# Transposing layer 1's input on VectorE and moving norms in a four-layer graph network

## The chip, the cores and the metric

The kernel runs on one core of a Trainium2 chip. The metric is the device time of one execution in microseconds. TensorE (PE) multiplies matrices and transposes through PSUM, VectorE (DVE), ScalarE (ACT) and GpSimd (POOL) do the elementwise work, and SyncE (SP) issues nearly all DMA transfers. Each of them works through its own queue of instructions in order.

## The reference

64 graphs of 256 nodes, 256 features, fp32. Four layers, each of the form "norm of x plus layer of x":

```python
x = _layernorm(x + L0(x, adj))   # gated recurrence over the 256 nodes
x = _layernorm(x + L1(x, adj))   # relu(D^-1/2 adj D^-1/2 (x W^T + b))
x = _layernorm(x + L2(x, adj))   # attention with relu projections, one head, mask adj
x = _layernorm(x + L3(x, adj))   # attention with 8 heads, mask adj > 0, output projection

def _layernorm(x, axis=-1, eps=1e-5):
    m = jnp.mean(x, axis=axis, keepdims=True)
    v = jnp.var(x, axis=axis, keepdims=True)
    return (x - m) / jnp.sqrt(v + eps)
```

The norms have no weights of their own.

## The kernel before

The recurrence of layer 0 runs first, for all 64 graphs together, and writes its states to `Hd` in HBM, laid out [node, graph, feature]. Then `_layers` does the residual and norm of layer 0 and the whole of layers 1 to 3, graph by graph. In it a graph's x is one tile `y` of 128 partitions by 2 by 256: node c*128 + p lies in partition p, half c.

`class Graph` holds one graph's steps. The steps of five graphs are interleaved by a list written out by hand, `ROUND`. In round t the letters stand for graphs at different depths: L is graph t+1, A is t, B is t-1, C is t-2 and E is t-3. So a graph passes the letters L, A, B, C, E in five rounds. The list sets the order on every engine, because the scheduler is switched off there (`tc.manual_schedule()`). At the head of each round the loads of graph t+2 are issued on SP:

```python
for t in range(-1, B + 3):
    if 0 <= t + 2 < B:
        graphs[t + 2].load()
    for step in ROUND:
        who, name, *args = step.split(".")
        b = t - "LABCE".index(who) + 1
        if 0 <= b < B:
            getattr(graphs[b], name)(*map(int, args))
```

The steps that matter here:

- `load` (L1033 to L1045): x into `xin`, adj into `ad`, adj once more in 32-wide blocks into `az` (eight DMAs of 32 KB), and the state from Hd into `y`. In `az` the blocks lie so that VectorE's transpose of 32 by 32 blocks (`adT_v`, L1076) gives the transposed adj.
- `residual_0` (L1049): y += xin on GpSimd.
- `norm_a`, `norm_b` (L949 to L961): mean and variance on VectorE, the power -1/2 on GpSimd (L953), `shift` = -mean * rstd on VectorE (L959), then y * rstd + shift in two halves on ScalarE (L961). The argument is the number of the layer whose sum is normed.
- `xT` (L987, L1094): the four 128x128 transposes of y on TensorE, and one copy of 128x512 out of PSUM on ScalarE. It is done for the inputs of layers 1, 2 and 3.
- `t` (L1099) and `g`: layer 1. t = xT^T W1^T + b1, then g, adj times t, with the degrees' scales, and y += g on GpSimd (L1108).
- `qk2`, `v2`, `s2` (L1140), `exp2`, `w2`, `pT2`, `f2`: layer 2.
- `bias_3` (L1176, L1177): y is written to `Yd` in HBM by a DMA, then b3 is added to y on GpSimd, in place. `Yd` is read only by a fallback that runs if a sum in layer 3 is out of range.
- `qk3`, `s3`, `v3`, `o3`, `d3`, `f3`: layer 3. `s3` issues 8 matmuls and then, four times, an add of the mask on VectorE (L1204), an exponential on ScalarE (L1205) and a sum of two halves on GpSimd (L1207, `p3s`). `o3` takes row sums from `p3s` (L1221) and the product with v (L1230).
- `store` (L1256): the DMA of y to the output.

PSUM tiles of the tag "mm" rotate through four buffers; `y` has seven buffers, `xin` and `az` three, `ad` four. A DMA takes one of eight semaphores in turn, and so waits for the DMA eight places ahead of it.

Of the kernel before, what the change touches and what calls it, by code (L numbers as in the profile page):

```python
# [9 lines left out]
F32 = mybir.dt.float32  # L10
BF16 = mybir.dt.bfloat16
AF = mybir.ActivationFunctionType
ALU = mybir.AluOpType
# [6 lines left out]
P = 128  # L20
# [891 lines left out]
def _layers(tc, ident, Hd, Yd, x, adj, weights, out):  # L912
# [8 lines left out]
    nc = tc.nc  # L921
    nat, W2, W3, b1_r, b2_r, b3_r, cols = weights
    B, N, D = x.shape
# [5 lines left out]
    with ExitStack() as ctx:  # L929
        const = ctx.enter_context(tc.tile_pool(name="l_const", bufs=1))  # L930
        W1T = const.tile([P, 2, D], F32, name="W1T")
# [7 lines left out]
        io = ctx.enter_context(tc.tile_pool(name="l_io", bufs=3))  # L939
# [4 lines left out]
        def norm_a(y, t):  # L944

            mv = small.tile([P, 2, 2], F32, tag="mv", name=f"mv_{t}")
            for c in range(2):
                st = small.tile([P, 6], F32, tag="st", name=f"st_{t}_{c}")
                nc.vector.bn_stats(st, y[:, c, :])  # L949
                nc.vector.bn_aggr(mv[:, c, :], st)  # L950
            rstd = small.tile([P, 2], F32, tag="rstd", name=f"rstd_{t}")
            nc.vector.tensor_scalar(rstd, mv[:, :, 1], EPS, None, ALU.add)  # L952
            nc.gpsimd.tensor_tensor(rstd, rstd, mhalf, ALU.pow)  # L953
            return mv, rstd

        def norm_b(y, mv, rstd, t):

            shift = small.tile([P, 2], F32, tag="shift", name=f"shift_{t}")
            nc.vector.scalar_tensor_tensor(shift, mv[:, :, 0], -1.0, rstd, ALU.mult, ALU.mult)  # L959
            for c in range(2):  # L960
                nc.scalar.activation(  # L961
                    y[:, c, :], y[:, c, :], AF.Identity, bias=shift[:, c:c + 1],
                    scale=rstd[:, c:c + 1],
                )

        def bank(name, shape=(P, 2, D)):
            return ps.tile(list(shape), F32, tag="mm", name=name, bufs=4)

        for c in range(2):
# [2 lines left out]
                nc.tensor.transpose(pt[:, k, :], nat[:, c, k * P:(k + 1) * P], ident)  # L972
            nc.vector.tensor_copy(W1T[:, :, c * P:(c + 1) * P], pt)

        nc.vector.tensor_copy(bv, cols[:, 4, :].unsqueeze(2).to_broadcast([P, 2, P]))
        pb = bank("bv3_ps", (P, D))
        for k in range(2):
# [4 lines left out]
        def flipped(src, t):  # L982

            pt = bank(f"tr_{t}")
            for a in range(2):
                for c in range(2):
                    nc.tensor.transpose(  # L987
                        pt[:, a, c * P:(c + 1) * P], src[:, c, a * P:(a + 1) * P], ident
                    )
            return pt  # L990

        def product(lhsT, rhs, t):

            pm = bank(f"mm_{t}")
            for c in range(2):
                for k in range(2):
                    nc.tensor.matmul(  # L997
                        pm[:, c, :], lhsT[:, k, c * P:(c + 1) * P], rhs[:, k, :],
                        start=(k == 0), stop=(k == 1),
                    )  # L1000
            return pm

        def new(tag, t, bufs=2, shape=(P, 2, D)):
            return work.tile(list(shape), F32, tag=tag, name=f"{tag}_{t}", bufs=bufs)

        def rows(b):
            return b.unsqueeze(1).to_broadcast([P, 2, D])
# [14 lines left out]
        class Graph:  # L1022
# [7 lines left out]
            def load(self):  # L1030
                b = self.b
                self.xin = io.tile([P, 2, D], F32, tag="xin", name=f"xin_{b}")
                nc.sync.dma_start(self.xin, x[b].rearrange("(c p) d -> p c d", p=P))  # L1033
                self.ad = io.tile([P, 2, N], F32, tag="ad", name=f"ad_{b}", bufs=4)
                nc.sync.dma_start(self.ad, adj[b].rearrange("(c p) m -> p c m", p=P))
                self.az = io.tile([P, 2, 8, 32], F32, tag="az", name=f"az_{b}", bufs=3)
                for j in range(4):
                    for a in range(2):
                        at = a * P + j * 32
                        nc.sync.dma_start(  # L1040
                            self.az[j * 32:(j + 1) * 32, a],
                            adj[b, :, at:at + 32].rearrange("(i r) c -> r i c", r=32),
                        )
                self.y = io.tile([P, 2, D], F32, tag="y", name=f"y_{b}", bufs=7)
                nc.sync.dma_start(self.y, Hd[:, b, :].rearrange("(c p) d -> p c d", p=P))  # L1045


            def residual_0(self):
                nc.gpsimd.tensor_add(self.y, self.y, self.xin)  # L1049

            def norm_a(self, l):
                self.mv = norm_a(self.y, f"{l}_{self.b}")

            def norm_b(self, l):
                norm_b(self.y, *self.mv, f"{l}_{self.b}")
# [37 lines left out]
                self.xT_sb = new(f"xT{l}", self.b)  # L1093
                nc.scalar.copy(self.xT_sb, pt)  # L1094

            def t(self):
                pm = product(self.xT_sb, W1T, f"t_{self.b}")
                self.t_sb = new("t", self.b)
                nc.vector.tensor_add(self.t_sb, pm, rows(b1_r))  # L1099

            def g(self):
                pm = product(self.adT_sb, self.t_sb, f"g_{self.b}")
# [155 lines left out]


        ROUND = """  # L1260
            A.xT.1 B.xT.2 E.o3 E.d3.0 B.qk2.0 C.norm_b.2 E.d3.1
            A.t B.qk2.1 B.v2 L.residual_0 B.masks L.degrees_a
            L.adT_v E.f3 L.degrees_b C.xT.3 L.adT_s A.g C.bias_3 L.norm_a.0
            C.qk3.0 C.qk3.1 E.norm_a.3 A.norm_a.1 L.norm_b.0 B.s2 B.exp2
            C.s3.0 C.v3 B.w2
            B.pT2 E.norm_b.3 E.store A.norm_b.1 C.s3.1 B.f2
            B.norm_a.2
        """.split()
        graphs = [Graph(b) for b in range(B)]
# [1 line left out]
# [6 lines that stand above are left out]
# [146 lines left out]
def kernel(ctx: ExitStack, tc: tile.TileContext, ins, out):  # L1423
# [25 lines left out]
    )  # L1449
    Yd = dram.tile([B, P, 2, D], F32, name="Yd")  # L1450
    found = _layers(tc, ident, Hd, Yd, x, adj, weights, out)
    with tc.If(found > 0):
        _layer_3(tc, ident, Yd, adj, l3, out)
# [36 lines left out]
```

## Time and profile before

| what | us |
|---|---|
| median of three runs | 3351.38 (3345.61 to 3360.14) |
| the profiled execution | 3353.51 |
| its span, first to last instruction | 3351.7 |
| recurrence ends, first load of `_layers` | 1475.4 |
| period of a round in the layers | 28.34 |

The page gives busy times of each engine and the span in 40 slices of about 84 us: the recurrence fills slices 1 to 17, the layers the rest. In the layers TensorE's clock was granted in full. A timeline lists instructions by their start; the number behind the start is the time from its first to its last instruction, where several are merged (x2, x4). "SPq" is the time in which SP issues a DMA, not the time of the transfer.

### The profile page before, as it was taken

To read this page: it belongs to the slowest core of one execution; us is meant where nothing else is said; L and a number is where in the kernel's file an instruction comes from. 1 tells how busy PE (TensorE), PEld (TensorE's weight loads), DVE (VectorE), ACT (ScalarE), POOL (GpSimd) and SP (SyncE) were. 2 spreads that over 40 slices of the span, in tenths; PEclk is the share of its full clock that TensorE was granted. 3 is DMA by queue.
4 is the path that set the end of the run, shared out by engine and by line. 5 is a ranking of instruction groups with operands and counts; after the bars stand their busy time and mean duration, and the time that the engine had idled before them with its cause. 6 is when DMAs were issued, how large, how long until landed. Compare 5 with 4: busy or idle time off the path is not lost.

```text
span 3351.7 us, 78940 instructions
## 1 busy us (share of the span) xinstructions
PE 3131.6 (93%) x28584; PEld 2311.5 (69%) x28584; DVE 2554.5 (76%) x7381; ACT 1838.6 (55%) x4754; POOL 1845.0 (55%) x2165
## 2 busy tenths in 40 slices
PE   5799998998879998969999999999999999999997
PEld 4566665555545555547888888888888888888885
DVE  3487777776667878856888888888888888888885
ACT  0155554544445544535666666666666666666664
POOL 2377777766667878833444444444444444444443
PEclk7899999999999999989999999999999999999999
DMA  9856685788877675241221211122222222222210
GB/s 292 247 161 156 168 194 152 179 198 207 204 181 178 163 174 152 65 105 47 56 57 54 57 56 54 54 55 58 57 58 58 58 57 58 57 58 58 58 33 20
DMA packets 528608, 364.62 MB, mean 109 GB/s; under 512 B 246620, under 2 KB 494568, under 8 KB 522984
## 3 DMA queue, kind: packets, MB, share of 16 engines
q1 hardware_dynamic: 510520, 342.63, 39.6%
q10 hardware_dynamic: 17696, 16.91, 1.5%
q8 instruction: 229, 3.75, 0.5%
q14 instruction: 163, 1.34, 0.1%
HBM read 240.78 MB, written 99.61 MB: 102 GB/s over the span
## 4 chain that ended last, share of the span: by engine, by line
PE 77%; DMA 8%; DVE 7%; issue 2%; SPq 2%; ACT 2%; POOL 1%; DVEq 0%; ACTq 0%; POOLq 0%
PE mm L997 14%; PE rc L605 6%; PE rc L597 4%; PE s L1195 4%; PE mm_2f L997 3%; PE mm_3v L997 3%; PE mm_3f L997 3%; PE mm_2v L997 3%; PE late L521 3%; PE mm_t L997 3%; PE mm_2s L997 3%; PE mm_g L997 3%; PE mm_2w L997 3%; PE o L1230 3%; DVE ACC L630 3%; PE o L1221 3%
## 5 line engine op out<-in xcount | busy, mean ns | idle before, releaser
L1207 POOL TENSOR_TENSOR p3s<-p 128x256 f32<-128x256 f32 x512 | 358.9, 733 | 364.7 <-ACT p L1205 364.6
L630 DVE SCALAR_TENSOR_TENSOR ACC<-keep,S,ACC 128x128 f32<-128x128 f32 x1712 | 479.1, 343 | 16.9 <-POOL ACC L876 11.2
L997 PE MATMUL mm<-xT,weights 128*128 128x256 f32 x2048 | 483.7, 384 | 2.7 <-ACT xT L1094 2.7
L997 PEld LDWEIGHTS mm<-xT,weights 128*128 128x128 f32 x2048 | 386.0, 191 | 79.9 <-issue 25.5
L1204 DVE TENSOR_TENSOR p<-s,neg 128x512 f32<-128x512 f32 x512 | 317.6, 682 | 118.2 <-PE s L1195 118.2
L667 POOL TENSOR_TENSOR ACC<-ACC,far 128x384 f32<-128x384 f32 (+1 forms) x313 | 372.1, 1189 | 24.5
L663 POOL TENSOR_TENSOR far<-hs,S 128x384 f32<-128x384 f32 (+1 forms) x313 | 304.7, 973 | 4.7
L1205 ACT ACTIVATE p<-p 128x512 f32<-128x512 f32 x512 | 292.4, 626 | 1.6 <-DVE p L1204 1.6
L961 ACT ACTIVATE y<-y,shift,rstd 128x256 f32<-128x256 f32 x512 | 272.9, 599 | 26.6 <-DVE shift L959 22.7
L597 PE MATMUL rc<-WxT,xqT 128*64 128x256 f32 x2048 | 274.8, 390 | 1.1 <-issue 1.1
L1119 ACT ACTIVATE qk<-mm,weights 128x256 f32<-128x256 f32 x256 | 107.5, 471 | 301.9 <-PE mm L997 301.9
L805 POOL TENSOR_TENSOR ready<-ACC,dinv 128x128 f32<-128x128 f32 x255 | 102.1, 400 | 304.7 <-DVE ACC L630 304.2
L1108 POOL TENSOR_TENSOR y<-y,g 128x512 f32<-128x512 f32 x64 | 81.0, 1266 | 301.8 <-issue 301.8
L1244 DVE RECIPROCAL rT<-o 128x256 f32<-128x256 f32 x128 | 223.7, 1748 | 0.3 <-PE o L1221 0.2
L949 DVE BATCH_NORM_STATS2 st<-y 128x6 f32<-128x256 f32 x512 | 209.6, 409 | 13.1 <-POOL y L1108 10.3
L521 PE MATMUL late<-Hw,An 64*32 64x256 f32 x3840 | 166.7, 400 | 42.1 <-DMA Hw<-hs 18.8
L605 PE MATMUL rc<-WhT,rT 128*64 128x128 f32 x2048 | 172.5, 290 | 35.6 <-DVE rT L828 33.2
L824 ACT ACTIVATE rs<-rc 128x128 f32<-128x128 f32 x256 | 71.1, 278 | 245.0 <-PE rc L605 245.0
L605 PEld LDWEIGHTS rc<-WhT,rT 128*64 128x64 f32 x2048 | 109.1, 138 | 133.2 <-DVE rT L828 110.8
L953 POOL TENSOR_TENSOR rstd<-rstd,mhalf 128x2 f32<-128x2 f32 x256 | 173.8, 697 | 47.9 <-DVE rstd L952 34.6
L1066 POOL TENSOR_TENSOR dis<-dis,mhalf 128x2 f32<-128x2 f32 x64 | 44.9, 702 | 273.2 <-DVE dis L1065 261.8
L605 PE MATMUL rc<-WhT,xpT 128*64 128x128 f32 x2048 | 169.4, 286 | 18.1 <-ACT xpT L614 18.1
(162 smaller groups left out, 7255.4 us busy)
## 6 DMA issues: line engine op xcount, KB each, us to landing
xX<-in_x_dram ACTq DMA_DIRECT2D x16, 1024.0 KB
Us<-xu SPq DMA_DIRECT2D x64, 256.0 KB
xq<-in_x_dram SPq DMA_DIRECT2D x64, 256.0 KB
ACC<-Us SPq DMA_DIRECT2D x32, 512.0 KB
Es<-eu SPq DMA_DIRECT2D x64, 256.0 KB
early_sb<-Es SPq DMA_DIRECT2D x32, 512.0 KB
xin<-in_x_dram SPq DMA_DIRECT2D x64, 256.0 KB
ad<-in_adj_dram SPq DMA_DIRECT2D x64, 256.0 KB
```

Of the source, the lines that this page charges most:

```text
L521: nc.tensor.matmul(pb[g][q * T:(q + 1) * T, e, :], An[rows, b].rearrange("p u s -> p (u s)"), Hw[rows, b, :], start=True, stop=True,)
L597: nc.tensor.matmul(G[o * B:(o + 1) * B], xqT[a, i // 2][:, i % 2, kc, h * B:(h + 1) * B], WxT[:, kc, o, gates], start=False, stop=False, s ...
L605: nc.tensor.matmul(G[o * B:(o + 1) * B], hT[:, kc * B:(kc + 1) * B], WhT[:, kc, o, g], start=False, stop=(kc == 1), skip_group_check=True,)
L630: nc.vector.scalar_tensor_tensor(acc[:, 0, :], keep[:, j % 2, :], s, acc[:, 0, :], ALU.mult, ALU.add)
L663: nc.gpsimd.tensor_mul(tmp[:, 0:count, :], hs.unsqueeze(1).to_broadcast(shape), s.unsqueeze(2).to_broadcast(shape),)
L667: nc.gpsimd.tensor_add(acc, acc, tmp[:, 0:count, :])
L961: nc.scalar.activation(y[:, c, :], y[:, c, :], AF.Identity, bias=shift[:, c:c + 1], scale=rstd[:, c:c + 1],)
L997: nc.tensor.matmul(pm[:, c, :], lhsT[:, k, c * P:(c + 1) * P], rhs[:, k, :], start=(k == 0), stop=(k == 1),)
L1204: nc.vector.tensor_add(p, s_ps[i], self.neg3)
L1205: nc.scalar.activation(p, p, AF.Exp, scale=ISQ)
L1207: nc.gpsimd.tensor_add(both, p[:, 0, :], p[:, 1, :])
L1244: nc.vector.reciprocal(rT, o_ps[:, 1, :])
```

## The change

Layer 1 no longer takes its transposed input from TensorE. The state and x are loaded a second and third time, in 32-wide blocks (`hz`, `xz`, eight DMAs each); GpSimd adds them (`residual_0`), and VectorE transposes the sum (`turn_0`) into `xT0`, before any norm. The norm is applied behind the product: W1 has its mean over the input features taken off once, at the start, so that the mean of x drops out, and t is the product times rstd, plus b1, in two halves with a scale per partition. y itself is still normed (`norm_b.0`), for the residual sum.

In ROUND the step A.xT.1 goes, A.t becomes A.t_a and A.t_b, L.turn_0 is new behind A.norm_b.1, and E.norm_b.3 with E.store move from ahead of A.norm_b.1 to behind C.s3.1.

```diff
+        mean = const.tile([P, P], F32, name="mean")
+        nc.gpsimd.memset(mean, 1.0 / D)
+        pb = bank("w1_mean", (P, D))
+        for k in range(2):
+            nc.tensor.matmul(pb, mean, W1T[:, k, :], start=(k == 0), stop=(k == 1))
+        for k in range(2):
+            nc.vector.tensor_sub(W1T[:, k, :], W1T[:, k, :], pb)
...
-                self.az = io.tile([P, 2, 8, 32], F32, tag="az", name=f"az_{b}", bufs=3)
-                for j in range(4):
-                    for a in range(2):
-                        at = a * P + j * 32
-                        nc.sync.dma_start(
-                            self.az[j * 32:(j + 1) * 32, a],
-                            adj[b, :, at:at + 32].rearrange("(i r) c -> r i c", r=32),
-                        )
+                self.az, self.hz, self.xz = (
+                    io.tile([P, 2, 8, 32], F32, tag=f"{s}z", name=f"{s}z_{b}", bufs=3)
+                    for s in "ahx"
+                )
+                for to, of in ((self.az, adj[b]), (self.hz, Hd[:, b, :]), (self.xz, x[b])):
+                    for j in range(4):
+                        for a in range(2):
+                            at = a * P + j * 32
+                            nc.sync.dma_start(
+                                to[j * 32:(j + 1) * 32, a],
+                                of[:, at:at + 32].rearrange("(i r) c -> r i c", r=32),
+                            )
...
             def residual_0(self):
                 nc.gpsimd.tensor_add(self.y, self.y, self.xin)
+                nc.gpsimd.tensor_add(self.hz, self.hz, self.xz)
+
+            def turn_0(self):
+                self.xT0 = new("xT0", self.b)
+                nc.vector.transpose(
+                    self.xT0.rearrange("p a m -> p (a m)"),
+                    self.hz.rearrange("p a i c -> p (a i c)"),
+                )
...
-            def t(self):
-                pm = product(self.xT_sb, W1T, f"t_{self.b}")
+            def t_a(self):
+                self.t_ps = product(self.xT0, W1T, f"t_{self.b}")
+
+            def t_b(self):
+
                 self.t_sb = new("t", self.b)
-                nc.vector.tensor_add(self.t_sb, pm, rows(b1_r))
+                for c in range(2):
+                    nc.vector.scalar_tensor_tensor(
+                        self.t_sb[:, c, :], self.t_ps[:, c, :], self.rstd0[:, c:c + 1], b1_r,
+                        ALU.mult, ALU.add,
+                    )
...
         ROUND = """
-            A.xT.1 B.xT.2 E.o3 E.d3.0 B.qk2.0 C.norm_b.2 E.d3.1
-            A.t B.qk2.1 B.v2 L.residual_0 B.masks L.degrees_a
+            B.xT.2 E.o3 E.d3.0 B.qk2.0 C.norm_b.2 E.d3.1
+            A.t_a A.t_b B.qk2.1 B.v2 L.residual_0 B.masks L.degrees_a
             L.adT_v E.f3 L.degrees_b C.xT.3 L.adT_s A.g C.bias_3 L.norm_a.0
             C.qk3.0 C.qk3.1 E.norm_a.3 A.norm_a.1 L.norm_b.0 B.s2 B.exp2
             C.s3.0 C.v3 B.w2
-            B.pT2 E.norm_b.3 E.store A.norm_b.1 C.s3.1 B.f2
+            B.pT2 A.norm_b.1 L.turn_0 C.s3.1 E.norm_b.3 E.store B.f2
             B.norm_a.2
         """.split()
```

More of the change, by code (lines that the diff above doesn't have):

```diff
@@ L1049, in residual_0 @@
                 nc.gpsimd.tensor_add(self.y, self.y, self.xin)
+                nc.gpsimd.tensor_add(self.hz, self.hz, self.xz)
[5 more added lines that the diff above has]
+                )
             def norm_a(self, l):
                 self.mv = norm_a(self.y, f"{l}_{self.b}")
+                if l == 0:
+                    self.rstd0 = self.mv[1]
             def norm_b(self, l):
```

## The prediction

> **What bounds the kernel now.** First the page: busy time and the slices.
>
> ```profile
> PE 3131.6 (93%) x28584; PEld 2311.5 (69%) x28584; DVE 2554.5 (76%) x7381; ACT 1838.6 (55%) x4754; POOL 1845.0 (55%) x2165
> ...
> PE   5799998998879998969999999999999999999997
> ...
> DMA  9856685788877675241221211122222222222210
> ```
>
> TensorE is full in slices 19 to 39: the layers, which the change touches. There the same pattern comes back every 28.34 us, one round (one graph enters, one leaves). The busy times of one round:
>
> ```profile
> core 0: us, PE busy (x) PEld busy (x) DVE busy (x) ACT busy (x) POOL busy (x), PEclk, DMA share, GB/s
> 2405.34:2433.68 28.34, 28.34 (x195) 22.90 (x194) 23.42 (x59) 18.32 (x41) 13.31 (x17) 1.00 0.21 56
> ```
>
> So a round ends when TensorE is through, and the reader would cut TensorE work. The chain of waits in one round shows what there is to cut:
>
> ```profile
> 2405.16 0.87 PE tr_x L987 x8
> 2406.04 0.57 PE o L1221 x8
> ...
> 2408.33 0.83 PE o L1221 x8
> ```
>
> The eight tr_x are the two transposes xT.1 and xT.2; four cost 0.435 us. The second row sum of o3 takes 0.83 instead of 0.57: 0.26 us of waiting for GpSimd's p3s.
>
> Then what is behind TensorE. SP's queue, one round:
>
> ```profile
> 2404.07 0.38 SPq L1256 DMA_DIRECT2D out_dram<-y  x1
> 2404.50 0.46 SPq L1033 DMA_DIRECT2D xin<-in_x_dram  x1
> 2405.07 0.45 SPq L1035 DMA_DIRECT2D ad<-in_adj_dram  x1
> 2405.56 3.91 SPq L1040 DMA_DIRECT2D az<-in_adj_dram  x8
> 2409.58 0.40 SPq L1045 DMA_DIRECT2D y<-Hd  x1
> 2412.97 0.37 SPq L1176 DMA_DIRECT2D Yd<-y  x1
> ```
>
> Loads stand behind the store of E, and the write of Yd stands behind the loads. The store waits for ACT's norm_b.3. The rest of the circle, in the timeline of the engines:
>
> ```profile
> 2422.39 1.27 POOL L1177 TENSOR_TENSOR y<-y,weights 128x512 f32<-128x512 f32 x1
> 2423.62 2.01 POOL L953 TENSOR_TENSOR rstd<-rstd,mhalf 128x2 f32<-128x2 f32 x3
> 2424.36 0.16 DVE L959 SCALAR_TENSOR_TENSOR shift<-mv,rstd 128x2 f32<-128x2 f32 x1 [0.51 <-POOL rstd L953]
> 2425.38 0.69 DVE L1140 TENSOR_TENSOR sm<-mm_2s,ad 128x512 f32<-128x512 f32 x1 [0.86 <-PE mm_2s L997]
> 2427.57 2.37 ACT L1205 ACTIVATE p<-p 128x512 f32<-128x512 f32 x4
> 2431.27 2.09 ACT L961 ACTIVATE y<-y,shift,rstd 128x256 f32<-128x256 f32 x4
> 2432.40 0.38 SPq L1256 DMA_DIRECT2D out_dram<-y  x1
> 2433.25 2.19 ACT L1205 ACTIVATE p<-p 128x512 f32<-128x512 f32 x4
> ```
>
> The add of b3 (L1177) overwrites y and so must wait until Yd has landed. Behind it in POOL's order stands L's rstd, behind that DVE's shift, behind that s2's multiply, and then exp2, s3.0's exponentials, the copies and norm_b.3, which releases the next store. **This circle is closed, and today it is slack**: store to end of loads 5.9 us, Yd's landing 2.04 (median in the trace's landing records), add start to s2 about 2.1 (2422.39 to 2424.36, plus the shift), s2 to the store 7.02 (2425.38 to 2432.40). With 0.15 for hand-overs 17.2 us of 28.34: 11.1 us free.
>
> **What the Trainium skill says.** "VectorE: DVE Perf Modes", The three transpose paths: VectorE transposes 32x32 blocks only, hence the block loads; the trace agrees, with eight loads ahead of an adTr of 711 ns for 128x512. "DMA: Bandwidth & Descriptors", Anatomy of one DMA: about 2 us are fixed, most of it until the last byte is confirmed (said of another issuing path); Yd's 2.04 agrees. Same page, Specifications: below 512 B a transfer is not at line rate; here a 128 B packet takes 13 ns and one of 1 KB 46 to 53, so a byte costs about twice as much. "SBUF — State Buffer", SBUF: two separate sides: VectorE and GpSimd lock each other out of a shared port pair; a 169 ns rstd (L952) at 2421.18 took 1.27 us, until GpSimd's add ended.
>
> **The change, part by part.**
>
> *Gains on TensorE.* A.xT.1 goes: 0.435 us. norm_b.3 (two of the four L961, 1.05 us) no longer stands ahead of s3.1's exponentials: these can start at 2432.37, when the first p is there, not at 2433.25, p3s ends about 0.9 us earlier, and the 0.26 us wait goes even though o3 comes 0.435 earlier. Next in line, qk2.0's xT.2 copy, is done some 0.4 us ahead of need. Sum 0.70: a round of 27.64 us if nothing else binds. ACT also loses a copy of 0.59.
>
> *VectorE.* turn_0 like adTr, 0.71, and up to 0.2 ahead of it for its eight waits; t as two halves at 0.488 (row L1159) for one of 0.686: +0.29. 23.42 becomes 24.4 of 27.6. turn_0 sits where VectorE idles 1.75 us before s3.1; the half copy delays f3's add by less than its 0.74 us of idling. Cost nothing; if that cover is gone, s3.1 is late by up to 0.9. A port lock of turn_0 against p3s was never seen: between 0 (adTr never varies beyond 711 to 715) and 0.7; I take 0.
>
> *GpSimd.* One add of 128x512, 1.27 us, in a stretch with 4.3 us idle behind it: nothing. W1's mean: two matmuls, two subtractions, a memset, while the layers' start waits for its first load: nothing.
>
> *SP's queue.* 16 more DMAs per graph, at the interval of az: 3.91/8 = 0.49 us each, **+7.9 us** between the store and Yd. The store itself comes later: norm_b.3 now stands behind norm_b.1 and four exponentials: ready after 1.04 + 2.08, **+3.1 us**. Together 11.0 of the 11.1 free. So before any friction the circle takes 28.2 us: the round of today. Two frictions:
> - Yd now follows y (256 KB) directly instead of by 2 us or more. ad, issued right behind xin, takes 3.32 to land where xin takes 2.95; y's packets need 16 x 53 ns per engine. Between 0 and 0.85; I take 0.4.
> - Rounds in which a 16 KB instruction fetch falls among the loads need about 7.0, not 5.9 (az 4.87 instead of 3.91 at 2433.90). 83 fetches of TensorE's queue fell into 55 rounds; by their place in the round about 0.6 per round fall into the longer window, at 1.05 us. 0 to 1.1; I take 0.6.
>
> The circle then takes 28.2 + 1.0 = **29.2 us**. Hd's 128 B pieces lie 64 KB apart, which no az shows: at worst each DMA takes twice its interval, +3.9 us; 1 KB pieces at that distance (y) land in 2.81 against 2.95 for xin, so I take 0.
>
> *Start.* y of graph 0 is issued behind 16 more DMAs (1480.40 today), of graph 1 behind 32: +7.9 and +15.8 us; GpSimd waited 10 us for the first. Rounds there are bound by waits, so some of the second is absorbed: between 5 and 16, I take +10.
>
> *Sum.* About 59 rounds both store and load: 59 x (29.2 - 28.34) = +51. Rounds outside the circle -2, start +10: +59 us on the profiled execution's 3353.5, which lies 2 us above the median: **3410**.
>
> **Rivals.**
> - *TensorE stays the bound* (faster): the circle closes within 27.64, so 63 x 0.70 = 44 us are gained, less 10: 3317. For it: full TensorE, cut in the right place, and estimates of slack summed from many rows. Against: it needs the 16 issues, the later store and both frictions to be 1.6 us cheaper than summed. It turns to faster from a circle below 27.9. Chance 0.12.
> - *The frictions do not appear* (no change): circle 28.2, 59 x -0.14 + 10 - 2: 3352. The circle from 27.9 to 28.5 belongs here. For it: every second round today has no stall. Against: a later window does not avoid the fetches. Chance 0.15.
> - *Hd's pieces are slow*: circle 33.1, 59 x 4.8 + 8: 3643. Against: y's landing. Chance 0.04.
> - *VectorE becomes the bound*: it needs 24.4 plus locks; to pass 28.34 it would have to lose 4 us more per round. Chance 0.01, inside the ranges above.
> - That xT.1 is not removed can be excluded: the order of instructions has four transposes fewer per graph.
>
> **How the numbers follow.** Half a per cent, 17 us, is about what a measurement here can tell from no change. Likeliest, 0.68: a circle of 28.5 to 29.9, 3368 to 3450. Slower 0.68 + 0.04 + 0.01 = 0.73, same 0.15, faster 0.12. The range takes in the no-change case and some of the faster one: 3335 to 3455.
>
> **What would show it.** Right: SP issues Yd straight after y with no gap; GpSimd's add of b3 waits for the DMA into Yd; DVE's shift of L waits longest for POOL's rstd; TensorE has idle time in slices 19 to 38; the period is above 28.5. Wrong: period 27.6, TensorE still full, Yd issued with a gap behind y. The 0.83 of o3 should be 0.57 where TensorE binds. If turn_0 takes over 0.71 or starts late behind GpSimd, the port lock was mis-sized.

## The result, and the profile after

The changed kernel takes 3476.42 us (median of four runs, 3469.24 to 3484.39) against 3350.70 before: a ratio of 1.0364, 95% interval 1.0339 to 1.0389. It is slower, as forecast, but by about twice the forecast 59 us, and above the stated range. The profiled execution took 3470.17 with a span of 3468.4, so the spans differ by 116.7 us. The page of the changed kernel, busy times, slices, and the chain that ended last by engine:

```profile
PE 3177.4 (92%) x28332; PEld 2323.2 (67%) x28332; DVE 2605.8 (75%) x7511; ACT 1818.7 (52%) x4690; POOL 1923.6 (55%) x2230
...
PE   5799999998888989859999999999999999999997
...
DMA  9757685877875754243333323332232333333310
...
PE 50%; DMA 12%; ACT 11%; DVE 10%; SPq 10%; POOL 4%; issue 3%; POOLq 0%; DVEq 0%; ACTq 0%
```

TensorE still looks full: 9 in every slice of the layers. Only the chain has changed: TensorE's part fell from 77% to 50%, that of SP's issuing rose from 2% to 10%. One round, from a store to the next, with the busy time and count of each engine:

```profile
core 0: us, PE busy (x) PEld busy (x) DVE busy (x) ACT busy (x) POOL busy (x), PEclk, DMA share, GB/s
2444.34:2474.58 30.24, 29.09 (x196) 22.89 (x190) 24.28 (x61) 18.01 (x40) 14.57 (x19) 1.00 0.30 70
```

The round is 30.24 us long instead of 28.34. TensorE counts as busy for 29.09 of it, although its work went down; experiment e1 below does the same TensorE work in 27.51. So part of its waiting is recorded as busy time, and the busy share hides it. SP's queue in the same round shows what fills it (start, time to issue, how many DMAs):

```profile
2444.34 0.38 SPq L1285 DMA_DIRECT2D out_dram<-y  x1
2444.77 1.34 SPq L1041 DMA_DIRECT2D xin<-in_x_dram  x1
2446.22 0.41 SPq L1043 DMA_DIRECT2D ad<-in_adj_dram  x1
2446.68 3.91 SPq L1052 DMA_DIRECT2D az<-in_adj_dram  x8
2450.63 3.91 SPq L1052 DMA_DIRECT2D hz<-Hd  x8
2454.59 3.90 SPq L1052 DMA_DIRECT2D xz<-in_x_dram  x8
2458.58 0.40 SPq L1057 DMA_DIRECT2D y<-Hd  x1
2459.09 0.40 SPq L1205 DMA_DIRECT2D Yd<-y  x1
2474.58 0.38 SPq L1285 DMA_DIRECT2D out_dram<-y  x1
```

SP issues without a pause from the store to Yd, and Yd follows y at once. In the kernel before there were 2.37 us between the two on average. GpSimd, which must not overwrite y before Yd has landed, now waits, and VectorE behind it (the waits from 1700 to 3200 us: total, times, longest):

```profile
DVE shift L959 <- POOL rstd L953: 178.4, 50, 5.1
POOL y L1206 <- DMA Yd<-y: 128.5, 43, 4.6
```

SP in its turn waits for ScalarE's norm before it can issue the next store (SP's own waits in the same stretch):

```profile
SPq L1285 <- ACT y L961: 750.6, 50, 16.1
```

In all of the first 58 rounds the add starts 0.13 us after Yd has landed, so it waits for Yd every time; the view names Yd 43 times. The chain of waits behind Yd in that round (start, duration):

```profile
2459.09 3.25 DMA Yd<-y
...
2462.47 1.27 POOL y L1206
2463.74 0.67 POOL rstd L953
...
2464.43 0.17 DVE shift L959
...
2464.62 1.09 ACT y L961 x2
2465.72 1.07 ACT sm L1026 x4
2466.78 2.28 ACT p L1234 x4
2469.06 0.47 ACT v L1211
```

Here L961 is norm_b of the graph that enters (layer 0), `sm` is exp2 and `p` the first exponentials of s3. Behind `v` and two more copies the view follows TensorE, since it traces the work that ended last in the whole program. The way to the next store is in ScalarE's timeline: norm_b.1, the second exponentials, norm_b.3.

```profile
2470.39 1.11 ACT L961 ACTIVATE y<-y,shift,rstd 128x256 f32<-128x256 f32 x2
2471.38 2.19 ACT L1234 ACTIVATE p<-p 128x512 f32<-128x512 f32 x4
2473.46 1.09 ACT L961 ACTIVATE y<-y,shift,rstd 128x256 f32<-128x256 f32 x2
```

Read with SP's queue this is the closed circle of the prediction: store, loads, Yd, the add of b3, rstd, shift, then ScalarE's work up to the norm that releases the next store. Its pieces, as means of the first 58 rounds, add up to the period: store to the end of y's issue 14.54, gap 0.12, Yd's landing 3.25, hand-over to GpSimd 0.13, add of b3 to s2 2.05, s2 to the store 10.09; together 30.18. The mean of the 58 intervals between stores is 30.177 (before 28.353).

A slower TensorE clock is not what makes the round long. In the changed kernel the granted clock fell to half in 23 of the 58 rounds, for 3.4 or 6.8 us; the 35 rounds without such a drop still take 30.01 us on average.

### The profile page after: what moved, and what is told of

Read it like the earlier page. It is cut to its first block, busy times and chain, and to the rows that moved or that the text cites. A ratio compares the mean times of both kernels' runs of the same rounds, so it can differ in the third digit from the quotient of the medians.

```text
span 3468.4 us, 79986 instructions
## 1 busy us (share of the span) xinstructions
PE 3177.4 (92%) x28332; PEld 2323.2 (67%) x28332; DVE 2605.8 (75%) x7511; ACT 1818.7 (52%) x4690; POOL 1923.6 (55%) x2230
## 4 chain that ended last, share of the span: by engine, by line
PE 50%; DMA 12%; ACT 11%; DVE 10%; SPq 10%; POOL 4%; issue 3%; POOLq 0%; DVEq 0%; ACTq 0%
SPq L1052 8%; PE rc L605 7%; PE mm L1005 7%; PE rc L597 5%; DMA Yd<-y 4%; ACT p L1234 4%; PE late L521 4%; PE mm_2f L1005 4%; DVE ACC L630 3%; PE z_ps L605 2%; PE z_ps L597 2%; ACT y L961 2%; POOL y L1206 2%; PE mm_2v L1005 2%; PE mm_t L1005 2%
## 5 line engine op out<-in xcount | busy, mean ns | idle before, releaser
L630 DVE SCALAR_TENSOR_TENSOR ACC<-keep,S,ACC 128x128 f32<-128x128 f32 x1712 | 479.1, 342 | 15.6 <-POOL ACC L876 9.9
L961 ACT ACTIVATE y<-y,shift,rstd 128x256 f32<-128x256 f32 x512 | 279.9, 598 | 239.6 <-DVE shift L959 239.3
L959 DVE SCALAR_TENSOR_TENSOR shift<-mv,rstd 128x2 f32<-128x2 f32 x256 | 101.9, 398 | 210.2 <-POOL rstd L953 210.2
L1005 PE MATMUL mm_2f<-w,pT 128*128 128x256 f32 x512 | 154.5, 454 | 49.1 <-ACT pT L1182 49.0
```

The costliest lines, as they stand in the source:

```text
L630: nc.vector.scalar_tensor_tensor(acc[:, 0, :], keep[:, j % 2, :], s, acc[:, 0, :], ALU.mult, ALU.add)
L961: nc.scalar.activation(y[:, c, :], y[:, c, :], AF.Identity, bias=shift[:, c:c + 1], scale=rstd[:, c:c + 1],)
L1005: nc.tensor.matmul(pm[:, c, :], lhsT[:, k, c * P:(c + 1) * P], rhs[:, k, :], start=(k == 0), stop=(k == 1),)
```

## Experiments

Periods below are means of the first 58 intervals between stores; landings and SP's stretches (store to the end of the last load's issue ahead of Yd) are means of the trace's records over the same rounds. The first four kernels ran on one chip (kernel before there: 3357.59), the other four on another (3355.76). Three theories were set against each other: T1, the closed circle through SP; T2, more work on VectorE and GpSimd; T3, the small packets of the new loads slow the transfers that others wait for. In the recorded expectations these are Theory 1 to 3.

| kernel | median us | ratio to before, 95% | period | first load to first store |
|---|---|---|---|---|
| before | 3350.70 | | 28.353 | 106.4 |
| after | 3476.42 | 1.0364 (1.0339 to 1.0389) | 30.177 | 122.0 |
| e1, sum apart | 3313.02 | 0.9866 (0.9830 to 0.9902) | 27.507 | 118.7 |
| e2, block loads behind Yd | 3316.68 | 0.9884 (0.9851 to 0.9918) | 27.507 | 117.9 |
| e3, y loaded first | 3430.98 | 1.0217 (1.0182 to 1.0252) | 29.412 | 118.3 |
| e4, norm back | 3363.98 | 1.0017 (1.0005 to 1.0030) | 28.340 | 116.0 |
| e5, loads alone | 3364.11 | 1.0023 (1.0015 to 1.0031) | 28.404 | 116.5 |
| e6, move alone | 3335.53 | 0.9933 (0.9915 to 0.9950) | 27.941 | 111.5 |
| e7, e1 and e2 and e3 | 3313.69 | 0.9869 (0.9847 to 0.9890) | 27.507 | 121.2 |
| e8, eight more loads | 3736.07 | 1.1117 (1.1087 to 1.1148) | 34.453 | 136.5 |

### e1: the sum with b3 in a tile of its own

```diff
                 nc.sync.dma_start(Yd[self.b], self.y)
-                nc.gpsimd.tensor_add(self.y, self.y, rows(b3_r))
+                y3 = io.tile([P, 2, D], F32, tag="y3", name=f"y3_{self.b}", bufs=3)
+                nc.gpsimd.tensor_add(y3, self.y, rows(b3_r))
+                self.y = y3
```

(`y` gets six buffers instead of seven; the new tile has three.) This opens the circle at one place, and keeps every load, every compute instruction and SP's order.

> The changed kernel, with one edit: the sum of y and b3 goes to a tile of its own instead of overwriting y, so GpSimd's add no longer waits for the DMA into Yd; every DMA and every instruction stays. Theory 1 (the closed circle store, loads, Yd, add of b3, s2, exponentials, store sets the round): the circle is cut, TensorE binds again, the round falls from 30.2 to about 27.6 us, 58 x 2.5 = 147 us less, about 3323. Theory 2 (the added work of VectorE and GpSimd fills the round): nothing changes, about 3470. Theory 3 (4096 more small packets per graph slow the transfers that others wait for): about 3470 too.

Measured: 3313.02, a period of 27.507. The add on GpSimd starts before SP has so much as issued Yd (timeline of e1):

```profile
2407.11 1.27 POOL L1207 TENSOR_TENSOR y<-y,weights 128x512 f32<-128x512 f32 x1
...
2407.51 0.40 SPq L1205 DMA_DIRECT2D Yd<-y  x1
```

and the chain of waits of a round is TensorE alone; the part around o3:

```profile
2415.68 1.92 PE mm_2f L1005 x8
2417.60 0.44 PE tr_x L995 x4
2418.04 0.57 PE o L1252 x8
2418.61 1.73 PE o L1261 x32
2420.34 0.43 PE o L1252 x8
```

Four transposes instead of eight, and no wait in o3. SP's stretch (14.62) and Yd's landing (3.26) are those of the changed kernel: both are as long as ever, but GpSimd's add no longer waits for them. The whole loss went with one write-after-read wait, while all the work of VectorE and GpSimd stayed: T2 falls. Of T3 one form is left, that the small packets make Yd itself land late; e3 and e6 decide it.

### e2: the new block loads behind Yd

```diff
-            L.adT_v E.f3 L.degrees_b C.xT.3 L.adT_s A.g C.bias_3 L.norm_a.0
+            L.adT_v E.f3 L.degrees_b C.xT.3 L.adT_s A.g C.bias_3 N.load_z L.norm_a.0
```

`load` keeps az and y; the loads of hz and xz for the same graph (N is graph t+2) are issued in `load_z`.

> The changed kernel, with the sixteen loads of hz and xz issued behind the write of Yd instead of ahead of it; the same DMAs, the same work on every engine. Theory 1: the circle loses 7.9 us of issuing and Yd no longer follows y directly, it closes in about 21 us, TensorE binds with a round of 27.6; the second graph's y also comes 8 us earlier at the start: 3315 to 3323. Theories 2 and 3: about 3470.

Measured: 3316.68 and the same period, 27.507. SP's queue of e2:

```profile
2419.57 4.00 SPq L1056 DMA_DIRECT2D az<-in_adj_dram  x8
2423.67 0.40 SPq L1050 DMA_DIRECT2D y<-Hd  x1
2424.19 0.38 SPq L1211 DMA_DIRECT2D Yd<-y  x1
2424.62 4.23 SPq L1056 DMA_DIRECT2D hz<-Hd  x8
```

Other than expected, Yd still follows y directly (it lands after 3.05 us), but 7.9 us of issuing are out of the way. A second cut of the same circle, at another place, gives the same round as the first.

### e3: y loaded first

```diff
+                self.y = io.tile([P, 2, D], F32, tag="y", name=f"y_{b}", bufs=7)
+                nc.sync.dma_start(self.y, Hd[:, b, :].rearrange("(c p) d -> p c d", p=P))
                 self.xin = io.tile([P, 2, D], F32, tag="xin", name=f"xin_{b}")
...
-                self.y = io.tile([P, 2, D], F32, tag="y", name=f"y_{b}", bufs=7)
-                nc.sync.dma_start(self.y, Hd[:, b, :].rearrange("(c p) d -> p c d", p=P))
```

The same 27 loads stand between the store and Yd, but Yd now follows a load of 32 KB and not one of 256 KB.

> The changed kernel, with y's load issued first in a graph's loads instead of last, so that Yd follows a 32 KB load of xz instead of the 256 KB of y. This sizes the term that the prediction put at 0.4 us. Theory 1: Yd lands some 2.4 us behind its issue instead of 3.2, the round falls by 0.8 to 29.4 us, 58 x 0.8 = 46 us, and the start gains some 6 to 8 us: about 3415. Theories 2 and 3: about 3465, by the start alone.

Measured: 3430.98; the period falls by 0.77 us to 29.412. SP's queue of e3:

```profile
2418.96 5.49 SPq L1054 DMA_DIRECT2D xz<-in_x_dram  x8
2424.56 0.38 SPq L1205 DMA_DIRECT2D Yd<-y  x1
```

and its wait for Yd (total, times, longest, from 1700 to 3150 us), still there but shorter:

```profile
POOL y L1206 <- DMA Yd<-y: 103.6, 41, 3.8
```

Yd lands 2.08 us after its issue instead of 3.25. That gives the price of Yd's neighbour by itself: about 1.2 us. The period shows 0.77 of it, since SP's stretch was 0.33 us longer here (14.87). All sixteen loads of small packets are still there, and Yd lands as fast as in the kernel before (2.05), so they do not make Yd late. The median stayed 16 us above the expected 3415; some 3 us of that are the start, which gained 3.8 us instead of 6 to 8, and the rest was not taken apart. The circle stays closed and longer than TensorE's 27.51. (In the profiled execution of e3 the recurrence ended 20.5 us later than in that of the changed kernel; its time of 3443.98 is the highest of the four. The period doesn't contain the recurrence.)

### e4: norm_b.3 and the store back where they were

```diff
-            B.pT2 A.norm_b.1 L.turn_0 C.s3.1 E.norm_b.3 E.store B.f2
+            B.pT2 E.norm_b.3 E.store A.norm_b.1 L.turn_0 C.s3.1 B.f2
```

> The changed kernel, with E.norm_b.3 and E.store put back ahead of A.norm_b.1 and C.s3.1; the loads and the transpose on VectorE stay. Theory 1: the store comes 3.1 us earlier, the circle closes in 27.1 us and no longer binds; but the exponentials of s3.1 are late again, and o3, now 0.44 us earlier, waits that much longer for p3s, so the round is that of the kernel before, 28.3: 3470 - 58 x 1.85 = about 3363. Theories 2 and 3: about 3470.

Measured: 3363.98 and a period of 28.340, within 0.02 us of before. Part of the chain of e4:

```profile
2442.51 1.09 ACT sm L1026 x4
2443.61 2.28 ACT p L1234 x4
...
2447.33 0.95 ACT y L961 x2
2448.28 0.42 issue
...
2452.05 0.73 POOL p3s L1236
2452.82 0.62 PE o L1250 x2
```

The four transposes are gone, yet nothing is gained: the norm (y L961) holds up the second set of exponentials, p3s comes when it came before, and TensorE waits in o3 for what the transposes used to cover. Without the move, removing xT.1 gained nothing. This also corrects the prediction's first reading of the kernel before: TensorE was not alone in setting the round there. The loop that sets e4's round, from mm_2s through the exponentials and p3s to o3 and back, is as long as the round before, and o3 waited for p3s there too, for 0.40 us (e6), recorded as busy time.

### e5: the kernel before with the 16 loads alone

```diff
-                for j in range(4):
-                    for a in range(2):
...
+                for to, of in ((self.az, adj[b]), (self.hz, Hd[:, b, :]), (self.xz, x[b])):
+                    for j in range(4):
+                        for a in range(2):
```

The new tiles are loaded and not read.

> The kernel before, with the sixteen loads of hz and xz added ahead of y and read by nothing; no other part of the change. Theory 1: the circle takes 17.2 + 7.9 us and some 1.5 of Yd behind y and fetches, 26.6, under the round of 28.3, so the rounds stay and only the start is later, by 10 to 15 us: about 3365. Theory 3 (small packets slow the transfers that others wait for): 3470, since they are all there. Theory 2: as before, 3353.

Measured: 3364.11, a period of 28.404. The loads alone lengthen SP's stretch to 14.87 and Yd's landing to 3.38, about as in the changed kernel. With the prediction's 2.1 and 7.02 us for the rest the circle takes 27.6 us, so under 1 us of slack is left, and GpSimd waits for Yd only in some rounds (from 1700 to 3100 us), for about a twelfth of the total of the changed kernel:

```profile
POOL y L1182 <- DMA Yd<-y: 10.5, 19, 1.7
```

### e6: the kernel before with the move alone

```diff
-            B.pT2 E.norm_b.3 E.store A.norm_b.1 C.s3.1 B.f2
+            B.pT2 A.norm_b.1 C.s3.1 E.norm_b.3 E.store B.f2
```

> The kernel before, with E.norm_b.3 and E.store moved behind C.s3.1 and nothing else. Theory 1: the circle grows by 3.1 us to 20.3 and does not bind; o3's wait for p3s of 0.26 us goes: round 28.08, 15 us less, about 3337. A rival that holds the later store itself for the loss expects slower than before.

Measured: 3335.53, 0.7% faster than before (0.5 to 0.85%), a period of 27.941. The chain around o3:

```profile
2402.57 0.87 PE tr_x L987 x8
2403.45 0.57 PE o L1221 x8
...
2405.74 0.43 PE o L1221 x8
```

The second row sum takes 0.43 where it took 0.83: the wait for p3s was 0.40, not 0.26. With the eight transposes still there, the move alone already gains 0.41 us per round, and the 0.43 from here to e1 is what the four transposes cost. Yd was issued directly behind y here too (gap 0.12), and landed after 3.28 us: the long landing needs no small loads. With e3 this ends T3.

### e7: e1, e2 and e3 together

> The changed kernel with the sum of y and b3 in a tile of its own, the loads of hz and xz behind Yd, and y's load first. Theory 1: the round stays at TensorE's 27.5 us, as with either of the first two alone; the start gains the 4 to 8 us by which y comes earlier: 3308 to 3315. It would be the best version, if the start can be seen at all.

Measured: 3313.69 with the period of e1 to the last digit. Once the circle is cut, a second and third cut add nothing. That y early in the queue would shorten the start was not borne out: first load to first store takes 121.2 us, against 118.7 in e1.

### e8: eight idle loads more

A fourth tile `idle` is loaded like `xz`, ahead of y, and not read.

```diff
-                for to, of in ((self.az, adj[b]), (self.hz, Hd[:, b, :]), (self.xz, x[b])):
+                for to, of in (
+                    (self.az, adj[b]), (self.hz, Hd[:, b, :]), (self.xz, x[b]), (self.idle, x[b]),
+                ):
```

> The changed kernel, with eight more loads of 32 KB (x in blocks once more, into a tile that nothing reads) ahead of y. Theory 1: each DMA ahead of Yd lengthens the round by its interval of issue: 8 x 0.49 = 3.9 us, and some 0.3 for fetches, a round of 34.4 instead of 30.2: 3470 + 58 x 4.2 = about 3714. Theory 2: 3470. Theory 3: in proportion to the packets, 2048 more on 4096 cost half of the 120 us again, about 3530.

Measured: 3736.07, a period of 34.453: +4.28 us for eight loads, 4.19 of them in SP's stretch (14.54 to 18.73). That is the round that T1 named; the time is 22 us above its 3714, most of it at the start, which the expectation had left out (136.5 us to the first store, against 122.0). The waits grow in the same places (from 1700 to 3100 us):

```profile
DVE shift L959 <- POOL rstd L953: 263.7, 41, 8.6
...
POOL y L1208 <- DMA Yd<-y: 229.3, 39, 8.1
```

While the circle binds, each microsecond of issuing is a microsecond of the round, which is what T1 says; T2 (3470) and T3 (3530) do not give this time.

## Why the prediction was right in kind and wrong in size

**Where the miss lies.** The forecast was +51 for the rounds and +8 for start and end. The spans give 58 x (30.177 - 28.353) = +105.8 for the rounds, +15.6 from the first load to the first store, +1.0 for the recurrence, -5.7 after the last of these rounds: 116.7. Of the 58 us that were missed, 55 lie in the length of the circle: 29.2 forecast, 30.18 measured. Term by term this 0.97 us is: Yd's landing +0.81, SP's stretch +0.14, hand-overs +0.10, the add of b3 to s2 -0.05, s2 to the store -0.03. The mechanism was the forecast one; the sizes were not, and one of them above all.

**The step that failed** is the friction "Yd now follows y directly", put at 0.4 with 0.85 as its upper bound. It measured 1.2: Yd landed in 3.25 us against 2.05 before. The bound was taken from y's own packets (16 x 53 ns per engine) and from ad behind xin, two loads. Neither measured the right thing: in the layers of the trace before, no write stood directly behind a load of equal size, and y's packets take longer than one engine's share. In the packet records (means of 48 rounds before, 45 after) the time from y's first packet to the end of its last is 1.47 us before and 1.71 after. Counted from Yd's issue, y's last packet ended 0.24 us ahead of it before, and now ends 2.23 us behind it. Yd's own packets ran from 0.87 to 1.69 us, and now run from 1.46 to 2.88. From there to the landing it is 0.36 to 0.37 us in both. So the whole 1.2 us is lost before Yd's last packet ends, in a stretch most of which y's packets still fill. e3 shows the term by itself (2.08 behind a small load), e6 shows it without the new loads (3.28). The term is 0.8 us too small, 46 us over 58 rounds. That descriptors on one DMA engine are consumed in ring order is in the Trainium skill ("DMA: Bandwidth & Descriptors", Queues, rings and completion order), and the trace agrees as far as it goes: Yd's first packet starts 0.6 us later than before, with 55% of y's packets ahead of it, and 43% of Yd's come behind the last of y's. The records do not tell the engine of a packet, so the order on one engine is not shown. Why y's packets take 1.7 us, where 16 of 53 ns make 0.85, was not tested and stays open.

**SP's stretch** was forecast at 5.9 + 7.9 + 0.6 = 14.4 and measured 14.54: the issue interval of 0.49 us held, and so did the instruction fetches in kind. In the 17 of the 58 rounds without a 16 KB fetch inside it the stretch averages 13.9 us, in the other 41 it averages 14.8. The remaining 0.14 us is worth 8 us.

**The move of the store** was forecast at 7.02 + 3.1 = 10.12 from s2 to the store and measured 10.09. The add of b3 to s2 was forecast at 2.1 and is 2.05. These terms stand.

**The start.** The 16 loads cost what was said: e5 puts the first store 10.0 us later, e4 9.5. e6, which has the move alone, puts it 5.0 us later, because the store itself stands further back in the round. The forecast had counted this only inside the circle. In the changed kernel the two make +15.6, and the 5.7 less at the end is about the move's part given back (e6 has 6.7 less there). What remains of the start in e2 and e7 (11 to 15 us, although y is issued early there) was not taken apart; in both, GpSimd's add of hz waits for xz.

**TensorE's side** was undervalued: 0.435 + 0.26 was forecast, 0.435 + 0.40 measured, so 27.51 and not 27.64. The 0.83 was compared with the other row sum's 0.57, but unhindered this row sum takes 0.43, in e1 and e6 alike. It didn't count here, since the circle was longer; in e1 it is the gain.

**Costed at nothing, and rightly:** turn_0 took 696 to 700 ns in 46 rounds of the layers. VectorE's timeline of the changed kernel around it:

```profile
2464.43 0.16 DVE L959 SCALAR_TENSOR_TENSOR shift<-mv,rstd 128x2 f32<-128x2 f32 x1 [4.26 <-POOL rstd L953]
2464.51 0.69 DVE L1169 TENSOR_TENSOR sm<-mm_2s,ad 128x512 f32<-128x512 f32 x1
...
2468.80 0.70 DVE L1066 STREAM_TRANSPOSE xT<-hz 128x512 f32<-128x512 f32 x1
```

The number in brackets is idle time and its releaser: 4.26 us of waiting for rstd, then s2, and turn_0 3.6 us after s2's end. In e1, where TensorE's work alone sets the round, turn_0 takes the same 698 ns (mean), so it delays nothing there either. Hd's 128 B pieces, 64 KB apart, were not slow: hz lands in 1.98 us (median), xz in 1.83. (The 2.04 us of Yd, which the prediction set beside a fixed cost of about 2 us, contain the moving of 256 KB; these loads of 32 KB, of another kind, take less.) So neither slow pieces of Hd nor VectorE's added work made the loss.

**Of the signs named beforehand,** four of five came as said: Yd straight behind y, GpSimd waiting for Yd, VectorE's shift waiting longest for rstd, a period over 28.5. The fifth, idle time of TensorE in its slices, came only in part: it is idle for 1.15 us of 30.24, 4%, which no digit shows, since a 9 begins at 90% busy. Its other waits are recorded as busy.

**A better version** is e1: one tile more and the same compute instructions, 1.3% faster than the kernel before (1.0 to 1.7%) and 163 us faster than the changed one. The change's two gains, 0.41 us by the move and 0.43 by the transposes, are both real, and were hidden behind a wait for one buffer of y.

## What to carry to other kernels

An in-order DMA queue joins everything that stands in it: before loads are put between a store and a later write, follow who waits for that write and whether this leads back to the store, and sum that circle against the period of the loop. A circle that only just fits is a warning, since a term that no row of the trace shows can then set the size of the loss, here 0.81 of the 0.97 us that were missed; give such a term a bound from its own kind of neighbour. If the circle closes over a write-after-read wait, a second buffer can cut it (here three buffers of a new tile for one of y); try that before giving the change up.

## What had not been expected of the hardware

- A write of 256 KB to HBM issued 0.5 us behind a load of 256 KB on the same queue lands after 3.25 us; 2.9 us behind it, after 2.05; 0.6 us behind a load of 32 KB, after 2.08. The long landing was the same in e1 and e6 (3.26, 3.28), and 3.38 in e5.
- Part of TensorE's waiting is recorded as busy: a round of the changed kernel has 29.09 us of busy TensorE, and e1 does the same work in 27.51.
- The recurrence, which no kernel here touched, ended up to 22.6 us apart between profiled executions, more than the spread of 14.5 us among the first three runs of the kernel before. Periods of the rounds repeated far better: three kernels gave 27.507.
